# A convolution, attention and Mamba kernel: z projected in slots 25 and 27 of a Mamba step, and the convolutions' raw weights fetched two pieces ahead into two buffers

## The chip, the cores and the metric

The program runs on one core of one Trainium2 chip. A core has five engines that run side by side, each in the order of its own instruction stream: PE (TensorE, matrix products), DVE (VectorE), ACT (ScalarE), POOL (GpSimd) and SP (SyncE, which here only issues DMAs). The engines wait for each other by semaphores, and the DMA engines move data between the device's memory and the on-chip memory. The metric is the time in microseconds (us) on the device for one execution; less is better.

## The reference

The reference computes two layers on an image of 64 x 64 positions with 256 channels, all in float32.

- Layer 0 normalises the image in groups, makes q by a 1x1, k by a 3x3 and v by a 5x5 convolution, applies a depthwise 3x3 convolution to all three, and does attention over the 4096 positions in 8 heads of 32 channels.
- Layer 1 is a Mamba block that runs forward and backward over the 4096 positions, a small two-layer network, and then a mixture of 8 experts with one routing for the whole image.

Two places of it matter here. In layer 0, the k and v convolutions:

```
qkv = concat([conv(x, W1, 0), conv(x, W3, 1), conv(x, W5, 2)])
```

In layer 1, each direction of Mamba:

```
xz = einsum('bld,ed->ble', x, in_proj_w);  xc, z = split(xz, 2)
xc = silu(conv1d(xc) + conv_b);  dt, B, C = split(xc @ x_proj_w)
dt = softplus(dt @ dt_proj_w + dt_proj_b)
h_t = exp(dt * A) * h_{t-1} + dt * B * xc;   y_t = h_t . C_t
out = (y + xc * Dp) * silu(z) @ out_proj_w
```

The half of the input projection called z is used only at the end, as a gate on y.

## The kernel before, in words

The program goes through four phases: the convolutions (`conv_phase`), attention, Mamba (`mamba_phase`) and the experts. Inside each phase every engine runs its instructions in exactly the order in which the Python code issues them (`tc.manual_schedule`), so an instruction that has to wait holds back all that stands behind it on its engine. A DMA is issued by an engine too: those of SP and those of POOL form two queues, and a DMA that has to wait for a buffer or for data holds its queue.

**The convolutions.** k and v are computed by a transform method along the rows (Winograd's): the image, the weights and the result are each transformed by sums and differences on DVE, and PE forms the products. PE takes the work in units: (k, half of the image, half of the output channels), later v and q in turn. A unit of k has 6 products of 12 matmul instructions, one of v 8 products of 20 (`feed`, lines 421 to 464). `transform_out` (line 473) takes the products from PSUM: for a pair, ACT copies the second one into a scratch tile `c` (line 481), and DVE forms sum and difference in `out_t`. PE may run at most three products ahead of DVE.

The weights come in pieces, one for each kind, half of the output channels and row dy of the filter. There are 3 pieces of 384 KB for each half of k and 5 pieces of 640 KB for each half of v. `load_raw` (line 279) fetches a raw piece through POOL's DMA queue, `weights` (line 285) transforms it on DVE in two (k) or three (v) groups of instructions, and after each group POOL's queue stores two results of 128 KB to the device's memory (line 293). SP fetches them from there when PE needs them (line 430). When all pieces of a half are through, `ready` lets PE's feeding function use them.

The first three pieces, the first half of k, are fetched at the very start, two into other buffers and one into the buffer that all later pieces use. The pool `rp` has one buffer for each tag (line 195), so there is one buffer for a raw piece. The later 13 pieces are walked through by the generator `all_weights` (line 658): it fetches the first piece when it is first entered, and each further one after the last group of the piece before. `step_fill` (line 675) takes groups of weights and of input transforms in turn, a fixed number after each group of products, so that they fill DVE's time between the products. The order of all instructions is thus fixed in Python; only the waits between engines depend on the chip.

**Mamba.** The 4096 positions are cut into 8 chunks of 512, and each is done in both directions, which gives 16 steps i. A step has 32 slots, one for each tile of 128 x 1024 values of the state: 4 groups e of channels, 4 groups k of the state's index, and j = 0 or 2. In slot n (line 1753 on) POOL makes dbx two slots ahead (`inflow`), ACT makes exp(dt * A) one slot ahead (`decay`) and copies the last state of the slot before (`keep`), a one-element addition on ACT brings in the carried state (`bring`, line 1702), DVE runs the scan and multiplies by C (`recur`, lines 1682 and 1687), and PE sums the state's indices for a finished pair of slots (`sum_states`, line 1719).

Between these, each slot advances a generator `prepare(q)` (line 1267) by one part; it makes what the next step needs. But for the first step, its first three parts stand in slots 29, 30 and 31 of the step two before q, its fourth in slot 0, and its last in slot 29 of step q - 1. So the parts of a loop near its end, with `at` = 0 to 5 (line 1344), stand in slots 24 to 29. In this loop, `dt_piece` finishes a part of dt on POOL and sends it through SP to the device's memory, from where it is read back in a broadcast form for the next step. In the parts at = 0 and 2, `in_pair` projects two blocks of 128 channels of z on PE (8 matmul instructions at line 1249) into both of the two PSUM buffers with the tag mm. In the parts at = 1 and 3, ACT copies them to a tile z (line 1354). At the end of part 3, `load_u` puts the fetch of the input of the step after into SP's queue (line 1258). The tile u has a single buffer, so that this fetch has to wait until PE is through with the projection of z. Part 1 of the next `prepare`, in slot 29, projects from the new u.

A generator `tail(c)` does the small network for a finished chunk beside all this. It says at every stop which engine it needs next, and it goes on in a slot only if that engine isn't marked as full there. The table `FULL` holds these marks, written by hand (line 1739); among PE's marks are the two slots in which z is projected. A tail starts in every second step and stretches over about two, so that it begins its last layer norm in slots 24 to 28 of an odd step i.

Of the kernel before, what the change touches and what calls it, by code (L numbers as in the profile page):

```python
# [14 lines left out]
FP = mybir.dt.float32  # L15
# [9 lines left out]
P = 128  # L25
H = W = 64
NT = H * W
C = 256
CT = C // P
# [8 lines left out]
ET = DI // P  # L38
# [31 lines left out]
def drain(gen):  # L70
    while step(gen):
        pass
# [101 lines left out]
def conv_phase(cx, xT, w1, w3, w5, temp, qd, kd, vd, uk, uv):  # L174
# [17 lines left out]
    with ExitStack() as ctx:  # L192
        one = ctx.enter_context(tc.tile_pool(name="a_one", bufs=1))
        up = ctx.enter_context(tc.tile_pool(name="a_u", bufs=3))
        rp = ctx.enter_context(tc.tile_pool(name="a_r", bufs=1))
# [70 lines left out]
        KS = {"k": 3, "v": 5}  # L266
# [11 lines left out]

        def load_raw(kind, co, dy, pool=rp, tag="wr"):
            n = KS[kind]  # L280
            r = pool.tile([P, 5, C], FP, name="wr", tag=tag)
            nc.gpsimd.dma_start(out=r[:, 0:n, :], in_=RAW[kind][co, :, :, dy, :].rearrange("x p c -> p x c"))
            return r

        def weights(kind, co, dy, r):
            s = tp.tile([P, 2, C], FP, name="wx", tag="t")
            x, y = s[:, 0, :], s[:, 1, :]
            w = [r[:, i, :] for i in range(KS[kind])]

            def pair(i):  # L290
                o = tp.tile([P, 2, C], FP, name="wo", tag="t")
                return o, lambda: [
                    nc.gpsimd.dma_start(out=UD[kind][co][i + v - 1][:, dy, :], in_=o[:, v, :]) for v in range(2)
                ]

            o, store = pair(1)
            plus(x, w[0], w[2])
            if kind == "v":
                plus(y, w[1], w[3])
                plus(x, x, w[4])  # L300
            plus(o[:, 0, :], x, y if kind == "v" else w[1])
            plus(o[:, 1, :], x, y if kind == "v" else w[1], ALU.subtract)
            store()
            yield
            for i in (3, 5) if kind == "v" else (3,):
                o, store = pair(i)
                w_ = w if i == 3 else w[::-1]
                if kind == "k":
                    madd(x, w_[2], 4.0, w_[0])
                    odd = w_[1]  # L310
                else:
                    madd(x, w_[4], 4.0, w_[2])
                    madd(y, w_[3], 4.0, w_[1])
                    madd(x, x, 4.0, w_[0])
                    odd = y
                madd(o[:, 0, :], odd, 2.0, x)
                madd(o[:, 1, :], odd, -2.0, x)
                store()
                yield
# [98 lines left out]
        ready, us, ms, where = set(), {}, {}, {}  # L418
# [185 lines left out]

        with tc.manual_schedule(engines=ORDERED):
            raw = [load_raw("k", 0, dy, accp, "acc") for dy in range(2)] + [load_raw("k", 0, 2)]
            mv = one.tile([P, CT, 2], FP, name="mv")
            stats = one.tile([P, CT, NCH, 6], FP, name="stats")
            for t in range(CT):
# [39 lines left out]
            for b in range(3):  # L649
                normalise(b)  # L650
            drain(weights("k", 0, 2, raw[2]))
            ready.add(("k", 0))
            first = inputs("k", 0)
            for _ in range(2):
                step(first)
            normalise(3)

            def all_weights(pieces):
                r = load_raw(*pieces[0])
                for n, p in enumerate(pieces):  # L660
                    yield from (True for _ in weights(*p, r))
                    if n + 1 < len(pieces):
                        r = load_raw(*pieces[n + 1])
                    if p[2] == KS[p[0]] - 1:
                        ready.add(p[0:2])

            fills = [
                first, all_weights([("k", 1, dy) for dy in range(3)]), inputs("k", 1),
                all_weights([("v", 0, dy) for dy in range(5)]), inputs("v", 0),
                all_weights([("v", 1, dy) for dy in range(5)]), inputs("v", 1),  # L670
            ]

            pure = fills[1::2]
# [492 lines left out]
def mamba_phase(cx, early, w_in, w_x, w_out, w1, w2, x1d, ud, bcd, dtd, x2d, u2d, usum):  # L1166
# [12 lines left out]
    with ExitStack() as ctx:  # L1179
# [81 lines left out]
        def in_pair(q, e):  # L1261
            return [in_proj(q % 2, gots[q]["u"], e), in_proj(q % 2, gots[q]["u"], e + 1)]
# [4 lines left out]
        def prepare(q):  # L1267

            d, got = q % 2, gots[q]

            ps = in_pair(q, 0)
            yield
            xp = early.wide("xp")
            nc.scalar.copy(xp[:, :, 0:3], halo[d])
            for v in range(2):
                nc.scalar.copy(xp[:, v, 3:], ps[v])
            ps = in_pair(q, 2)
            yield
            for v in range(2):
                nc.scalar.copy(xp[:, 2 + v, 3:], ps[v])  # L1280
            nc.scalar.copy(halo[d], xp[:, :, N : N + 3])
            for _ in range(4):
                yield

            xc = None
            for e in range(ET + 1):
                if e > 0:
                    xc = got["xc"] = xc or pr.tile([P, ET, N], FP, name="xc", tag="xc")
                    nc.scalar.activation(xc[:, e - 1, :], ps, AF.Identity, bias=cx.col(f"convb{d}", e - 1))
                if e < ET:  # L1290
                    ps = mm_psum()
                    for k in range(4):
                        nc.tensor.matmul(  # L1293
                            ps, taps[d][:, 4 * e + k, :], xp[:, e, k : k + N], start=k == 0, stop=k == 3
                        )
                yield
            nc.scalar.activation(xc, xc, AF.Silu)
            yield
            ps = mm_psum()
            nx = DR + 2 * DS  # L1300
            for e in range(ET):
                nc.tensor.matmul(ps[0:nx, :], wx[d][:, e, :], xc[:, e, :], start=e == 0, stop=e == ET - 1)
            yield
            xd = few()[0:nx, :]
            nc.scalar.copy(xd, ps[0:nx, :])

            at = 0 if d else DR
            nc.sync.dma_start(out=bcd[q], in_=xd[at : at + 2 * DS, :])
            yield


            r = slice(32 * d, 32 * d + DR)
            ex = dt = None
            for e in range(ET + 1):
                if e > 0:
                    ex = early.wide("ex")[:, :, 0:N] if e == 1 else ex
                    dt = dt or sp.tile([P, ET, N], FP, name="dt", tag="dt")
                    nc.scalar.activation(ex[:, e - 1, :], ps, AF.Abs, bias=cx.col(f"dtb{d}", e - 1))
                    nc.scalar.activation(dt[:, e - 1, :], ps, AF.Relu, bias=cx.col(f"dtb{d}", e - 1))
                if e < ET:  # L1320
                    ps = mm_psum()
                    nc.tensor.matmul(ps, wdt[r, P * e : P * e + P], xd[r, :], start=True, stop=True)
                yield

            nc.scalar.activation(ex, ex, AF.Exp, scale=-1.0)
            yield
            rds, sums = {}, {}
            for e in range(ET + 2):
                if e < ET:
                    rd = rds[e] = few()  # L1330
                    nc.scalar.activation(rd, ex[:, e, :], AF.Identity, scale=-1.0, bias=-1.0)
                    nc.scalar.add(rd, rd, 1.0)
                if e > 1:
                    nc.scalar.copy(dt[:, e - 2, :], sums.pop(e - 2))
                if 0 < e <= ET:
                    ps = sums[e - 1] = mm_psum()
                    for v, x in enumerate((rds.pop(e - 1), ex[:, e - 1, :], dt[:, e - 1, :])):
                        nc.tensor.matmul(ps, cx.ident, x, start=v == 0, stop=v == 2)
                yield

            nc.scalar.activation(ex, ex, AF.Ln, bias=1.0)
            yield
            got["dt"] = dt
            for at, (v, e) in enumerate(((0, 0), (1, 0), (0, 1), (1, 1), (0, 2), (0, 3))):
                dt_piece(q, v, e, ex)
                if at == 4 and q > 1:
                    load_first(q, 0)
                if at in (0, 2):
                    zs = in_pair(q, ET + at)
                if at in (1, 3):  # L1350
                    z = sp.tile([P, 2, N], FP, name="z", tag="z", bufs=3)
                    got.setdefault("z", []).append(z)
                    for f in range(2):
                        nc.scalar.copy(z[:, f, :], zs[f])
                if at == 3 and q + 1 < 2 * NCH:
                    load_u(q + 1)
                yield
# [367 lines left out]
        def close(i, e):  # L1725
# [11 lines left out]
        LATE = {0: 0, 1: 0, 2: 0, 3: 0, 4: 0, 7: 5, 13: 2, 14: 2, 15: 2, 16: 2}  # L1737

        FULL = {
            "PE": {0, 1, 2, 3, 4, 5, 6, 7, 9, 18, 19, 20, 21, 24, 26, 29, 30},  # L1740
            "ACT": {0, 6, 7, 8, 16, 17, 18, 19, 20, 21, 22, 23, 30, 31},
            "POOL": {0, 1, 2, 4, 24, 25, 26, 27, 28, 29, 30, 31},
            "DVE": {8, 16},
# [3 lines left out]
        with tc.manual_schedule(engines=ORDERED):  # L1747
# [5 lines left out]
            for n, (i, e, k, j) in enumerate(slots):  # L1753
                at = n % SPS
# [391 lines left out]
```

## Time and profile before

| What | Value |
| --- | --- |
| Median of 3 runs | 4312.76 us (4305.44 to 4313.22) |
| Profiled execution, its own time | 4316.87 us |
| Its span, first to last instruction | 4315.0 us |
| PE busy | 3617.0 us (84%) |
| DVE busy | 3482.8 us (81%) |
| ACT busy | 2675.4 us (62%) |
| POOL busy | 1775.7 us (41%) |
| Granted TensorE clock, mean | 0.913 |
| Convolutions | 0 to about 725 us |
| Attention | about 725 to 2040 us |
| Mamba | about 2040 to 4000 us |
| Experts | about 4000 to 4315 us |

The profile is of one execution, so durations and waits are of that one, and sums are made against its own time. A line of a group says: source line, engine, operation, tile written and tiles read, shapes and count, then busy us and mean ns of one, then the idle time of the engine just before these instructions, with what ended it. A line of a time line says: start in us, length in us, engine, source line, operation, tiles, count, and in brackets the idle time before it with what ended it. SPq and POOL lines with a DMA operation are issues: the transfer itself goes on after them. Of several things that an instruction waits for, the profile names the one that came last by its own account, which can be the wrong one.

### The profile page before, as it was taken

The numbers are of one execution on the slowest core, as the hardware profiler recorded it, in microseconds if no ns is written. First come the engines' busy times: TensorE is split into PE (matmuls) and PEld (weight loads), VectorE is DVE, ScalarE is ACT, GpSimd is POOL, SyncE is SP. The second block draws the span as 40 slices with busy tenths as digits, with TensorE's granted clock in tenths as the row PEclk, the third lists the DMA queues.
The fourth block names the chain that finished last, engine by engine and source line by source line (L and its number), as shares of the span: only waits on it lengthen the run. The fifth ranks groups of instructions, "written<-read, shape, count | busy, mean of one in ns | idle before, by whom it ended". The sixth has DMA issues, their size and how long they took to land. (4 is left out here: it accounts for less than half of the span.)

```text
span 4315.0 us, 43522 instructions
## 1 busy us (share of the span) xinstructions
PE 3617.0 (84%) x15080; PEld 1184.1 (27%) x15080; DVE 3482.8 (81%) x2882; ACT 2675.4 (62%) x4176; POOL 1775.7 (41%) x1148
## 2 busy tenths in 40 slices
PE   4659895999999999998778787878888787876798
PEld 2214341222222222222222222222222222221343
DVE  6887876888888879778899998999999989999211
ACT  1012123888788788776777777777877777774122
POOL 2210000000000000000888888888888889897000
PEclk9879996999999999999888898989899898987799
DMA  4322124000000000002333433433334434432121
GB/s 148 126 81 90 68 91 130 4 20 22 21 26 11 25 22 21 11 18 84 106 114 114 125 121 114 128 114 117 110 106 122 128 114 121 121 110 85 64 64 38
DMA packets 150532, 351.18 MB, mean 81 GB/s; under 512 B 35493, under 2 KB 44453, under 8 KB 150046
## 3 DMA queue, kind: packets, MB, share of 16 engines
q1 hardware_dynamic: 139214, 313.17, 23.6%
q0 software_dynamic: 11088, 35.14, 2.4%
q8 instruction: 120, 1.97, 0.2%
q14 instruction: 110, 0.90, 0.1%
HBM read 268.69 MB, written 79.56 MB: 81 GB/s over the span
## 5 line engine op out<-in xcount | busy, mean ns | idle before, releaser
L1671 POOL TENSOR_TENSOR dbx<-dtxr,b 128x1024 f32<-128x1024 f32 x512 | 1202.1, 2359 | 202.6 <-DVE da L1682 125.4
L959 ACT ACTIVATE e<-sc 128x1024 f32<-128x1024 f32 x1024 | 992.8, 1023 | 205.6 <-PE sc L952 161.4
L1682 DVE TENSOR_TENSOR_SCAN da<-da,state,dbx 128x1024 f32<-128x1024 f32 x416 | 976.7, 2348 | 113.5 <-ACT dbx L1702 66.4
L880 DVE TENSOR_TENSOR s<-s,e 128x1024 f32<-128x1024 f32 x768 | 880.4, 1214 | 43.9 <-ACT e L959 43.3
L1661 ACT ACTIVATE da<-dtr,aneg 128x512 f32<-128x512 f32 x1024 | 708.1, 692 | 59.9 <-DVE h L1682 27.7
L952 PE MATMUL sc<-q,kS 32*128 32x512 f32 x4096 | 653.9, 644 | 21.3 <-DMA kS<-kd 11.5
L132 POOL TENSOR_TENSOR ln_few<-ln_few,minus_half 128x4 f32<-128x4 f32 x29 | 29.4, 1013 | 1415.7 <-DMA ln_few<-ln_row 1415.7
L887 PE MATMUL av<-e,vT 128*32 128x512 f32 x4096 | 549.6, 608 | 3.7 <-ACT o L893 3.7
L1687 DVE TENSOR_TENSOR h<-da,c 128x1024 f32<-128x1024 f32 x416 | 509.4, 1225 | 34.5 <-PE y L1719 4.0
L452 PE MATMUL cv<-v,u 128*128 128x512 f32 x928 | 420.8, 614 | 63.7 <-DVE pad L272 27.2
L1719 PE MATMUL y<-h,sel 128*32 128x512 f32 x2048 | 374.0, 653 | 100.9 <-DVE h L1687 73.5
L1249 PE MATMUL mm<-u,win 128*128 128x512 f32 x496 | 271.8, 704 | 96.3 <-DMA u<-ud 83.9
L952 PEld LDWEIGHTS sc<-q,kS 32*128 32x128 f32 x4096 | 211.3, 184 | 467.7 <-issue 243.4
L452 PEld LDWEIGHTS cv<-v,u 128*128 128x128 f32 x928 | 181.5, 198 | 301.5 <-issue 229.8
L528 DVE SCALAR_TENSOR_TENSOR acc<-pad,wdw_s,acc 128x768 f32<-128x768 f32 (+1 forms) x192 | 244.5, 1279 | 19.4 <-ACT acc L524 13.3
L1682 DVE TENSOR_TENSOR_SCAN h<-da,state,dbx 128x1024 f32<-128x1024 f32 x96 | 224.9, 2343 | 15.5 <-ACT da L1661 6.3
L1692 POOL TENSOR_TENSOR h<-h,c 128x1024 f32<-128x1024 f32 x96 | 226.1, 2355 | 2.1 <-ACT state L1710 2.1
L1293 PE MATMUL mm<-xp,taps 128*128 128x512 f32 x480 | 213.7, 597 | 11.2 <-DVE m L1440 11.2
L1710 ACT COPY state<-da 128x2 f32<-128x2 f32 x415 | 65.3, 157 | 241.4 <-DVE h L1687 240.6
L880 DVE TENSOR_TENSOR s<-e 128x1024 f32<-128x1024 f32 x128 | 150.7, 1217 | 72.1 <-ACT e L959 71.9
L887 PEld LDWEIGHTS av<-e,vT 128*32 128x32 f32 x4096 | 81.3, 108 | 396.8 <-issue 379.2
L1249 PEld LDWEIGHTS mm<-u,win 128*128 128x128 f32 x496 | 108.4, 227 | 267.2 <-issue 147.8
(347 smaller groups left out, 3822.8 us busy)
## 6 DMA issues: line engine op xcount, KB each, us to landing
dtr<-dtd SPq DMA_DIRECT2D x128, 512.0 KB
dtxr<-dtd SPq DMA_DIRECT2D x128, 512.0 KB
b<-bcd SPq DMA_DIRECT2D x64, 256.0 KB
c<-bcd SPq DMA_DIRECT2D x64, 256.0 KB
dtd<-dt SPq DMA_DIRECT2D x64, 256.0 KB
dtd<-few SPq DMA_DIRECT2D x64, 256.0 KB
u<-uv SPq DMA_DIRECT2D x24, 640.0 KB
u<-ud SPq DMA_DIRECT2D x16, 512.0 KB
```

The lines of the kernel that those rows point to most:

```text
L452: nc.tensor.matmul(rows4(ps), u[:, dy, P * ci : P * ci + P], v[:, dy : dy + HR, ci, :], start=dy + ci == 0, stop=dy == k - 1 and ci == CT - 1,
L528: nc.vector.scalar_tensor_tensor(o, src, w_ap, o, ALU.mult, ALU.add)
L880: nc.vector.tensor_tensor(z, x, y, ALU.add)
L887: nc.tensor.matmul(g.av[32 * h : 32 * h + 32, :], vT[:, kb, P * t + 32 * h : P * t + 32 * h + 32], es[h // 2][:, h % 2, :], start=kb == 0, ...
L952: nc.tensor.matmul(ps[h // 2][:, h % 2, :], kS[r, t, P * kb : P * kb + P], q_t[r, t, :], start=True, stop=True,)
L959: nc.scalar.activation(e, ps[i], AF.Exp)
L1249: nc.tensor.matmul(ps, win[d][:, t, P * e : P * e + P], u[:, t, ::-1] if d else u[:, t, :], start=t == 0, stop=t == CT - 1,)
L1661: nc.scalar.activation(da[:, v, :], dts[i, e, j][0][:, v, :], AF.Exp, scale=aneg[i % 2][:, a : a + 1])
L1671: nc.gpsimd.tensor_tensor(u, dts[i, e, j][1], bcs[i, k][0][:, None, :].to_broadcast([P, 2, N]), ALU.mult)
L1682: nc.vector.tensor_tensor_scan(das[n].rearrange("p v n -> p (v n)"), da.rearrange("p v n -> p (v n)"), u.rearrange("p v n -> p (v n)"), st ...
L1687: nc.vector.tensor_tensor(h, da, bcs[i, k][1][:, None, :].to_broadcast([P, 2, N]), ALU.mult)
L1719: nc.tensor.matmul(ys[i, e][32 * j : 32 * j + 32, :], cx.sel, hs[n + j // 2][:, j % 2, :], start=False, stop=k == SQ - 1,)
```

## The change

In the convolutions, the tag of the raw pieces gets two buffers in the pool `rp`. A list `ahead` holds the pieces that are fetched and not yet used. One of the 13 later pieces is fetched at the very start, behind the first three; a second one after the third piece has been transformed. From then on each piece that has been transformed is followed by the fetch of the piece two after it, over the borders between the halves and kinds as well. The order of all DVE instructions stays.

In Mamba, the parts that project z move from at = 0 and 2 to 1 and 3 (slots 25 and 27), and the parts that copy it from 1 and 3 to 2 and 4 (slots 26 and 28). The fetch of the next u stays at the end of part 3, which now also holds the second projection of z, ahead of it. In `FULL`, PE's marks move from slots 24 and 26 to 25 and 27.

```diff
-            r = pool.tile([P, 5, C], FP, name="wr", tag=tag)
+            r = pool.tile([P, 5, C], FP, name="wr", tag=tag, bufs=2 if pool is rp else None)
...
             raw = [load_raw("k", 0, dy, accp, "acc") for dy in range(2)] + [load_raw("k", 0, 2)]
+            pieces = [("k", 1, dy) for dy in range(3)] + [("v", co, dy) for co in range(CT) for dy in range(5)]
+            ahead = [load_raw(*pieces.pop(0))]
...
             drain(weights("k", 0, 2, raw[2]))
+            ahead.append(load_raw(*pieces.pop(0)))
...
-            def all_weights(pieces):
-                r = load_raw(*pieces[0])
-                for n, p in enumerate(pieces):
-                    yield from (True for _ in weights(*p, r))
-                    if n + 1 < len(pieces):
-                        r = load_raw(*pieces[n + 1])
-                    if p[2] == KS[p[0]] - 1:
-                        ready.add(p[0:2])
+            def all_weights(kind, co):
+
+                for dy in range(KS[kind]):
+                    yield from (True for _ in weights(kind, co, dy, ahead.pop(0)))
+                    if pieces:
+                        ahead.append(load_raw(*pieces.pop(0)))
+                ready.add((kind, co))
...
-                if at in (0, 2):
-                    zs = in_pair(q, ET + at)
                 if at in (1, 3):
+                    zs = in_pair(q, ET + at - 1)
+                if at in (2, 4):
                     z = sp.tile([P, 2, N], FP, name="z", tag="z", bufs=3)
...
-            "PE": {0, 1, 2, 3, 4, 5, 6, 7, 9, 18, 19, 20, 21, 24, 26, 29, 30},
+            "PE": {0, 1, 2, 3, 4, 5, 6, 7, 9, 18, 19, 20, 21, 25, 27, 29, 30},
```

More of the change, by code (lines that the diff above doesn't have):

```diff
@@ L656, in conv_phase @@
             normalise(3)
-            def all_weights(pieces):
-                r = load_raw(*pieces[0])
-                for n, p in enumerate(pieces):
-                    yield from (True for _ in weights(*p, r))
-                    if n + 1 < len(pieces):
-                        r = load_raw(*pieces[n + 1])
-                    if p[2] == KS[p[0]] - 1:
-                        ready.add(p[0:2])
+            def all_weights(kind, co):
[4 more added lines that the diff above has]
+                ready.add((kind, co))
             fills = [
-                first, all_weights([("k", 1, dy) for dy in range(3)]), inputs("k", 1),
-                all_weights([("v", 0, dy) for dy in range(5)]), inputs("v", 0),
-                all_weights([("v", 1, dy) for dy in range(5)]), inputs("v", 1),
+                first, all_weights("k", 1), inputs("k", 1),
+                all_weights("v", 0), inputs("v", 0),
+                all_weights("v", 1), inputs("v", 1),
             ]
```

## The prediction

> **What bounds the kernel now.** I read the page first (span 4315.0 us), then the busy time by stage, because no engine is full all the way. Columns: us, then busy us and count of PE, PEld, DVE, ACT, POOL, then granted TensorE clock, DMA share, GB/s.
>
> ```profile
> 0.00:310.00 310.00, 164.29 (x340) 67.34 (x341) 238.72 (x395) 36.93 (x50) 65.09 (x125) 0.82 0.37 122
> 310.00:725.00 415.00, 344.30 (x851) 144.68 (x849) 319.28 (x299) 91.47 (x136) 26.16 (x53) 0.90 0.22 76
> ...
> 2040.00:4000.00 1960.00, 1547.65 (x4342) 504.41 (x4341) 1779.27 (x1077) 1440.47 (x2799) 1662.59 (x947) 0.88 0.38 115
> ```
>
> The convolution's first 310 us and the Mamba phase belong to DVE; the convolution from 310 us leans on PE. The two halves of the change fall into the two DVE stages. For the first I asked for the groups up to 450 us; the line below is the first instruction of a weight piece:
>
> ```profile
> L275 DVE TENSOR_TENSOR wx<-wr 128x256 f32<-128x256 f32 x26 | 10.1, 419 | 39.5 <-DMA wr<-in_w 33.6 <-issue 5.9
> ```
>
> DVE stands still 39.5 us because a raw piece has not landed. The time line of DVE has the nine places (start, length, idle before):
>
> ```profile
> 77.98 0.42 DVE L275 TENSOR_TENSOR wx<-wr 128x256 f32<-128x256 f32 x1 [4.76 <-DMA wr<-in_w]
> ...
> 96.95 0.76 DVE L275 TENSOR_TENSOR wx<-wr 128x256 f32<-128x256 f32 x2 [3.09 <-DMA wr<-in_w]
> ...
> 105.17 1.29 DVE L275 TENSOR_TENSOR out_t<-cv,c 128x512 f32<-128x512 f32 x2 [2.48 <-ACT c L481]
> ...
> 161.29 0.76 DVE L275 TENSOR_TENSOR wx<-wr 128x256 f32<-128x256 f32 x2 [5.99 <-DMA wr<-in_w]
> ...
> 209.79 0.76 DVE L275 TENSOR_TENSOR wx<-wr 128x256 f32<-128x256 f32 x2 [5.90 <-issue]
> ```
>
> The others are 85.14 (4.69), 149.50 (0.52), 222.31 (1.49), 235.20 (7.08) and 269.83 (5.96). The "issue" one is the same line and has the same size. The time line of POOL, then of PE, shows why a fetch is late and where PE is the judge:
>
> ```profile
> 73.18 1.07 POOL L293 DMA_DIRECT2D uk<-wo  x2 [9.39 <-DVE wo L272]
> 74.24 0.75 POOL L282 DMA_DIRECT2D wr<-in_w  x1
> ```
> ```profile
> 91.80 43.61 PE L452 MATMUL cv<-v,u 128*128 128x512 f32 x96 [13.89 <-DMA u<-uk]
> ```
>
> The fetch follows the last store of the piece before, so DVE sees its whole flight (3.6 to 8.3 us to landing, median 4.8).
>
> For Mamba I took the time lines around the end of a step (slot = one scan). Step 5, SP queue, ACT and DVE; step 4, PE:
>
> ```profile
> 2761.11 0.63 SPq L1379 DMA_DIRECT2D dtd<-few  x1
> 2763.02 0.32 SPq L1258 DMA_DIRECT2D u<-ud  x1
> ```
> ```profile
> 2761.31 0.58 ACT L1354 COPY z<-mm 128x512 f32<-128x512 f32 x1 [2.10 <-PE mm L1249]
> 2763.02 0.58 ACT L1354 COPY z<-mm 128x512 f32<-128x512 f32 x1 [1.13 <-PE mm L1249]
> ```
> ```profile
> 2766.18 2.36 DVE L1682 TENSOR_TENSOR_SCAN da<-da,state,dbx 128x1024 f32<-128x1024 f32 x1 [1.92 <-ACT dbx L1702]
> ...
> 2778.77 2.36 DVE L1682 TENSOR_TENSOR_SCAN da<-da,state,dbx 128x1024 f32<-128x1024 f32 x1 [1.72 <-ACT dbx L1702]
> ```
> ```profile
> 2633.11 3.70 PE L1249 MATMUL mm<-u,win 128*128 128x512 f32 x8
> ...
> 2647.32 2.90 PE L1249 MATMUL mm<-u,win 128*128 128x512 f32 x3 [7.10 <-DMA u<-ud]
> ```
>
> Two waits per step: scan 29 waits because ACT stands in the second pair of z copies, and the next step's first scan waits for a chain: u fetched, next step's in-projection on PE, its xp copies on ACT, decay and dbx behind them.
>
> **What the Trainium skill says.** "DMA: Bandwidth & Descriptors", Rules for kernel authors: issue a DMA early and wait on it late, and its fixed cost overlaps; that is the first half of the change. The same page, Anatomy of one DMA, puts a GpSimd-issued DMA at about 2.0 us plus bytes / 436 GB/s: an estimate of 3.5 us for 640 KB. The trace's 4.8 median is used. The section adds that a semaphore wait is held by the issuing sequencer, not by the DMA engines: so a u fetch that waits on PE holds SP's later fetches, as the trace shows at 2763.02. "TensorE: Matmul & The Clock Gate", Part 1: an idle window of about 3.4 us halves the clock. The trace agrees: after the 13.89 us wait the granted clock is 0.50 from 91.8 to 96 us and 1.00 from 98.
>
> **The raw weights, step by step.** Pieces p0 to p2 are ("k",1), p3 to p7 ("v",0), p8 to p12 ("v",1). Removed: no DVE work, only waits. Added: one fetch in flight and 5 KB a partition.
> - Start: one more 384 KB fetch among the input loads, with the queues at 370 to 406 GB/s up to 18 us: at most 1.0 us later; bn_stats already waits for the last loads. I take +0.7 (0 to 1.0).
> - p1 (61.5 to 77.98): fetched at 33, no wait, -4.76. p2's fetch leaves where p1's left (74.24) and lands near 78; p1 now ends at 73.2 + 2.4 = 75.6, so p2 still waits 2.3. Gain here 4.76 + 4.69 - 2.3 = 7.1.
> - p3: its wait of 3.09 goes, but the next instruction, out_t at 105.17, waits for PE's second product. ACT's wait before it is put down to a store, yet 24 matmuls of 0.45 us from 91.80, with some 2 us lost at half clock, end at 104.5: PE. PE starts when p2's transformed weights are back, 7.1 earlier. So the 3.09 turns into wait for PE: gain 0.
> - p6 0.5, p7 6.0, p9 5.9, p10 1.5, p11 7.1, p12 6.0. Each fetch now leaves a whole piece earlier; the tightest is p7's, out at about 137.6 on the new clock and needed at 147.7, against 8.3 us for the slowest flight. What follows each finds its product: PE is idle before these (18.31 us at 216.18, 17.45 at 272.98, both for DVE). Sum 27.0.
> - The POOL queue gets no new wait: a fetch needs the buffer of the piece just finished, whose last store stands just ahead of it. Six scratch buffers of tag t still suffice: a store lands 2.0 us after issue, its buffer returns at least 6 us later.
>
> Sum: -7.1 - 27.0 + 0.7 = -33.4. From 298 us PE works on what DVE delivers (22.00 us wait there for pad), so the shift passes through the PE-led part unshortened.
>
> **z one slot later.** Work is equal; 15 steps (0 to 14) prepare a successor. Even steps: no tail work for PE lies at slots 24 to 27, so PE's order is the same; z's first eight matmuls stay. Their two copies (1.1 us) go behind keep, decay and dbx of the next slot, so the second eight start near 2634.6 instead of 2633.11 and end near 2638.5. The u fetch (same slot 27, now behind z in the same call) leaves at 2640.91 anyway, since it is queued behind the dtd stores that POOL releases at 2640.06: about 2 us of cover. Gain 0. If the cover is gone, each us costs 14 us in all (14 fetches of u). SP's b, c, first_r and dtr/dtxr fetches are queued behind it; ACT and POOL need them in the next step.
>
> Odd steps with a tail (3, 5, 7, 9, 11, 13): FULL now lets the tail's PE work (L113, after DVE's m) go at slot 24, before z instead of between its pairs. I estimate PE at step 5: L113 from 2750.4, z1 from 2752.5, y sums, z2 about 2758 to 2762 (was 2759.3 to 2763.0); u leaves up to 1.2 earlier, at some steps 0.2. The z copies stand behind decay and dbx of slot 29, so the wait before scan 29 (1.70 to 1.95 in these six, 10.7 in all) goes. But the next step's first scan still waits for the u chain: DVE arrives 1.8 earlier and waits that much longer, less u's gain. I take 0.5 x 6 = -3, bounded by -11 (the whole wait stays away) and +6 (1 us late in six).
>
> Total -33.4 - 3 = -36.4. Against the profiled execution, 4316.87 (span 4315.0, 1.9 around it): 4280.5. The runs' median lies 4.1 lower at 4312.76: **4276**.
>
> **Rivals.**
> 1. Mamba keeps more: the u chain has slack and the 10.7 stays won, 4312.8 - 33.4 - 10.7 = 4269. For it: step 13 has no wait at the next first scan. Against: the other five wait 0.75 to 2.1 there.
> 2. PE becomes the bound in the convolution, as it does for p3: half of the later 27 turns into waits for products, 4312.8 - 7 - 13.5 + 0.7 - 3 = 4290. For it: 105.17 already waits. Against: PE's idle gaps of 8.4 to 22 us afterwards.
> 3. Slower: z's second pair falls in a cold clock. Matmuls then take twice the time (3.7 becomes 7), it starts 2 us later, and u leaves 3 or more after its old time; 14 x 3.2 = 45 eats the 36: 4321. It decides from 36.4 / 14 = 2.6 us of lateness a step to break even. Against: the idle gap before it is 1 to 2 us, under the window.
> 4. The fetches stay late (the second buffer is not free when wanted) and nothing is gained: about 4312. Against: its reader is the piece just done.
>
> **How the numbers follow.** Forecast 0.68, rival 1 0.12, rival 2 0.10, rival 3 0.06, rival 4 0.04. Two tenths of a per cent (8.6 us, about what runs of this kernel can tell) gives faster 0.90, same 0.04, slower 0.06. The range, 4265 to 4293, holds most of the forecast (4268 to 4286), rival 1's upper half and rival 2.
>
> **What would show it.** Idle before wx<-wr falls from 39.5 to 2 or 3 us; out_t near 98 us waits some 5.6 for ACT c; the 17.45 and 22 us waits of PE shrink by their share of 27; the convolution ends 33 earlier. In Mamba no wait before scan 29 in odd steps, a longer one before the next first scan, u leaving no later. Wrong if waits on wr remain beyond p2, if DVE's waits for c grow beyond p3's, or if u leaves later in even steps.

## The result, and the profile after

The changed kernel takes 4273.62 us (median of 4 runs, 4266.57 to 4276.95) against 4312.93 for the kernel before beside it (4 runs, 4305.44 to 4313.22). The ratio is 0.9914, with an interval of 0.9901 to 0.9928: 37 us (31 to 43) less by the ratio. On another chip the same two kernels gave 0.9917 (0.9900 to 0.9934). The forecast was 4276.

The profiled execution after took 4276.95 us, its span is 4275.1 us. The stages by busy time come first, cut where the same work begins and ends (columns as for before):

```profile
0.00:277.00 277.00, 157.06 (x334) 64.95 (x334) 232.56 (x391) 34.86 (x46) 65.11 (x125) 0.84 0.42 136
277.00:692.00 415.00, 346.47 (x858) 145.92 (x856) 322.48 (x290) 92.75 (x140) 25.07 (x51) 0.91 0.21 72
...
2007.00:3967.00 1960.00, 1556.01 (x4372) 507.36 (x4371) 1787.54 (x1089) 1446.58 (x2809) 1663.48 (x948) 0.88 0.38 116
```

The first stage is 33 us shorter with nearly the same work in it: DVE is busy 232.6 of 277 us where it was busy 238.7 of 310. The groups of instructions up to 450 us have the wait itself:

```profile
L275 DVE TENSOR_TENSOR wx<-wr 128x256 f32<-128x256 f32 x26 | 10.0, 417 | 2.7 <-DMA wr<-in_w 2.7
```

39.5 us of idle time before these instructions became 2.7. The time line of DVE shows the one wait for a raw piece that is left, p2's, and the place that stood at 105.17 before:

```profile
80.64 0.42 DVE L275 TENSOR_TENSOR wx<-wr 128x256 f32<-128x256 f32 x1 [2.68 <-DMA wr<-in_w]
...
105.31 1.29 DVE L275 TENSOR_TENSOR out_t<-cv,c 128x512 f32<-128x512 f32 x2 [10.30 <-ACT c L481]
```

p2 waits 2.68 (2.3 was forecast). But the transform at 105.31 starts no earlier than before, after a wait of 10.30 instead of 2.48: in this pair of profiles the first 7 us gained are lost again there. The time line of PE shows the same start as before (91.80), and where the gain appears later:

```profile
91.79 43.77 PE L452 MATMUL cv<-v,u 128*128 128x512 f32 x96 [11.53 <-DMA u<-uk]
...
245.66 3.78 PE L444 MATMUL cv<-xpad,wq 128*128 128x512 f32 x4 [13.67 <-DVE out_t L275]
271.44 3.78 PE L444 MATMUL cv<-xpad,wq 128*128 128x512 f32 x4 [22.01 <-DVE pad L272]
```

The third group of matmuls of the q convolution ("q's third group" from here on) stands at 271.44, where it stood at 298.76: 27.3 earlier, against 27.0 that the forecast had for the pieces from p6 on. Its wait is still put down to DVE, and the last product of the convolution ends 28.4 earlier (635.3, before 663.7).

POOL's queue tells why PE got nothing out of the first 7 us in this pair. The lines are issues, uk<-wo the stores of transformed weights, wr<-in_w the raw fetches:

```profile
79.48 0.88 POOL L282 DMA_DIRECT2D wr<-in_w  x1
81.82 0.56 POOL L293 DMA_DIRECT2D uk<-wo  x1 [1.46 <-DVE wo L275]
82.67 1.60 POOL L293 DMA_DIRECT2D uk<-wo  x3 [0.29 <-DVE wx L272]
84.26 0.87 POOL L282 DMA_DIRECT2D wr<-in_w  x1
```

p2's stores leave at 81.8, 4.5 earlier than before (86.33), but now behind p3's raw fetch of 640 KB, issued at 79.48, and with p4's right after them. The trace's answer for the tile uk from 81 to 98 us gives the time from a store's issue to its landing, for before and for after:

```profile
DMA to landing us min/median/max: 2.0/2.0/2.8
```
```profile
DMA to landing us min/median/max: 3.1/3.4/4.1
```

The first of p2's stores lands at 85.91, 4.1 after its issue (before: 88.34, 2.0 after). SP then fetches u at 86.03, and PE starts 5.76 later; before, it was 88.45 and 3.35. So 4.5 us of lead shrink to 2.4 at the landing and to nothing at PE. Two passages of the Trainium skill, "DMA: Bandwidth & Descriptors", fit: within one queue of a DMA engine descriptors start in order (section Two DMAs through the same engine are not ordered), so a small store has a large fetch ahead of it; and the DMA engines go round between queues packet by packet (section Queues, rings and completion order), so the fetch of u shares them with p4. No run here shows the order inside a queue or the turns of an engine. What the traces show is the load: between 82 and 92 us the queues moved 289 GB/s after, 167 before. In the 3 us from about the first fetch of u on, SP's queue, which carries u, moved 0.23 MB after (86 to 89 us) and POOL's 0.61; before it was 0.46 and 0.27 (88.4 to 91.4 us).

For Mamba, step 5 again, at its end: DVE, SP's queue, ACT and PE (PE: the tail's L113, the second z projection, the next step's in-projection).

```profile
2730.70 2.33 DVE L1685 TENSOR_TENSOR_SCAN da<-da,state,dbx 128x1024 f32<-128x1024 f32 x1
...
2745.10 2.36 DVE L1685 TENSOR_TENSOR_SCAN da<-da,state,dbx 128x1024 f32<-128x1024 f32 x1 [3.55 <-ACT dbx L1705]
```
```profile
2728.26 0.43 SPq L1382 DMA_DIRECT2D dtd<-few  x1
2729.51 0.32 SPq L1260 DMA_DIRECT2D u<-ud  x1
```
```profile
2730.29 1.05 ACT L1357 COPY z<-mm 128x512 f32<-128x512 f32 x2
```
```profile
2716.87 2.79 PE L113 MATMUL tl<-m,mean_mat 128*128 128x512 f32 x4 [2.89 <-DVE m L1483]
...
2725.77 3.70 PE L1251 MATMUL mm<-u,win 128*128 128x512 f32 x8
...
2736.11 9.94 PE L1251 MATMUL mm<-u,win 128*128 128x512 f32 x16 [3.72 <-ACT da L1664]
```

Scan 29 (2730.70) has lost its wait of 1.92, since ACT's z copies at 2730.29 now stand behind decay and dbx. But u leaves only when z's second projection is through (2729.47), so it leaves 1.1 after the start of scan 28, as before, and the next first scan waits 3.55 instead of 1.72. In this step the wait has moved and little is won, as forecast. In the even step 4 the second projection of z ends at 2604.5 and u leaves at 2607.16, right behind the dtd stores, with 2.6 us of cover (forecast: about 2).

From profile to profile the 39.9 us build up so: -28.4 at the end of the convolution, -24.4 at Mamba's first scan, -43.3 at Mamba's last scan, -39.9 at the end. The 4 us lost in and around attention are within the scatter of that stretch: the changed kernel's own two profiles (e10 has the second) have 1384.8 and 1375.9 us for it. The -18.9 in Mamba can't be believed as it stands either: see the experiments.

### The profile page after: what moved, and what is told of

Read it like the earlier page. It is cut to its first block, busy times and chain, and to the rows that moved or that the text cites. A ratio compares the mean times of both kernels' runs of the same rounds, so it can differ in the third digit from the quotient of the medians.

```text
span 4275.1 us, 43538 instructions
## 1 busy us (share of the span) xinstructions
PE 3614.0 (85%) x15080; PEld 1184.8 (28%) x15080; DVE 3484.1 (81%) x2882; ACT 2674.4 (63%) x4176; POOL 1775.6 (42%) x1148
## 5 line engine op out<-in xcount | busy, mean ns | idle before, releaser
L1251 PE MATMUL mm<-u,win 128*128 128x512 f32 x496 | 262.1, 683 | 94.8 <-DMA u<-ud 59.1
```

Of the source, the lines that this page charges most:

```text
L1251: nc.tensor.matmul(ps, win[d][:, t, P * e : P * e + P], u[:, t, ::-1] if d else u[:, t, :], start=t == 0, stop=t == CT - 1,)
```

## The experiments

Three sets, each on one chip with the kernel before beside it. "After" is the changed kernel.

### The two halves, and the halves of the second (e1 to e4)

e1 has the raw weights' half alone, e2 the whole Mamba half alone. e3 moves z but leaves FULL as it was; e4 moves only PE's marks in FULL:

e1, the core of its edit (the fetches as in the diff of the change; Mamba as before):

```diff
-            r = pool.tile([P, 5, C], FP, name="wr", tag=tag)
+            r = pool.tile([P, 5, C], FP, name="wr", tag=tag, bufs=2 if pool is rp else None)
...
+            ahead = [load_raw(*pieces.pop(0))]
```

e3, which is e2 without its line in FULL:

```diff
-                if at in (0, 2):
-                    zs = in_pair(q, ET + at)
                 if at in (1, 3):
+                    zs = in_pair(q, ET + at - 1)
+                if at in (2, 4):
```

e4, which is e2's line in FULL alone:

```diff
-            "PE": {0, 1, 2, 3, 4, 5, 6, 7, 9, 18, 19, 20, 21, 24, 26, 29, 30},
+            "PE": {0, 1, 2, 3, 4, 5, 6, 7, 9, 18, 19, 20, 21, 25, 27, 29, 30},
```

> The raw weights' half alone (two buffers, two pieces ahead), z and FULL as before. Theory A (the trace after: the convolution gives 27 to 28, Mamba the rest): q's third group of matmuls at 271 to 272 us, the convolution's end near 635, 27 to 28 us less than before in all, Mamba's 16 steps as long as before (1946 us from first to last scan, odd steps 736). Theory B (the prediction as written): 33 us less. Theory C (raw weights change Mamba too, by moving it in time): Mamba shorter than 1940.

> The Mamba half alone (z in slots 25 and 27, FULL's marks with it). Theory A: 10 to 13 us less than before, all in the six odd steps with a tail (736 to about 724), no wait before scan 29 there, u's flight 7.8 to about 5.8 us. Theory B: 3 us less; the u chain takes the gain back. Theory D (the two profiles differ by chance of 10 us in Mamba): between.

> z in slots 25 and 27, but FULL's marks stay at 24 and 26, so that the tail's work stays where it was and the x2d store still leaves some 9 to 10 us after scan 24 begins. Theory E (the earlier tail frees the DMA queues for u): scan 29's waits of 1.7 to 1.9 go, u's flight stays near 7.8, the wait before the next first scan grows, gain 0 to 4 us. Theory F (the z copies out of ACT's way are what counts): gain 9 to 12 us as with both.

> Only FULL's marks move, z stays in slots 24 and 26: the tail's products, its x2d store and its norm come a slot earlier. Theory E: u's flight in odd steps falls from 7.8 to about 6, gain 5 to 10 us, scan 29's waits mostly stay or shrink as z's second pair comes earlier on PE. Theory F: u's flight as before, gain under 3 us.

| Kernel | Median, us | Ratio to before (4306.22, 52 runs) | In us |
| --- | --- | --- | --- |
| e1, raw weights alone | 4274.22 | 0.9925 (0.9912 to 0.9939) | -32 (-38 to -26) |
| e2, z and FULL | 4301.26 | 0.9989 (0.9981 to 0.9997) | -5 (-8 to -1) |
| e3, z without FULL | 4311.77 | 1.0009 (1.0001 to 1.0017) | +4 (0 to +7) |
| e4, FULL alone | 4297.61 | 0.9983 (0.9975 to 0.9990) | -7 (-11 to -4) |

The halves add up: -32 and -5 make -37, the whole change's ratio gives -37. Nearly all of it is the raw weights. In the Mamba half the named act, moving z, doesn't pay by itself; what pays is the new marks, by which the tail may use PE in slots 24 and 26 and no longer in 25 and 27. The intervals of e2 and e4 overlap; by the means of their 21 and 16 runs e2 is 4.0 us slower (0.7 to 7.3), so moving z costs a little on top of the marks.

Of the expectations, e1's interval holds both the 27 to 28 of Theory A and the 33 of Theory B. e2 rules out Theory A's 10 to 13. e3 came out slower, where both of its theories had a gain or nothing. e4 gains what Theory E said, but the part of E that u's flight stays near 7.8 without the marks failed: e3 has 6.0.

In the trace, e1 has the convolution of after: q's third group at 270.55, idle time before wx<-wr 2.6. For Mamba the four profiles, those of before and after, and those of later runs give the following; the six steps are the odd ones from 3 to 13, all in us:

| Profile of | Waits before scan 29, six steps | Waits at the next first scan, six steps | Length of the six steps | First to last scan |
| --- | --- | --- | --- | --- |
| before | 10.7 | 6.7 | 736.1 | 1945.7 |
| before again (e9) | 10.2 | 0.3 | 732.0 | 1929.5 |
| e1 (Mamba as before) | 11.0 | 2.0 | 729.3 | 1933.8 |
| e3, z without FULL | 0 | 6.4 | 725.0 | 1929.6 |
| e2, z and FULL | 0 | 7.4 | 725.0 | 1931.7 |
| after | 0 | 4.8 | 724.1 | 1926.8 |
| after again (e10) | 0 | 2.8 | 719.6 | 1927.0 |
| e4, FULL alone | 0 | 2.9 | 718.5 | 1918.5 |
| e8, raw weights and FULL | 0 | 2.6 | 723.9 | 1930.3 |
| e11, the same | 0 | 8.1 | 728.3 | 1928.5 |

Three things follow. First, either edit takes the whole wait before scan 29 away. With FULL alone the tail's L113 no longer holds up z's second projection: that ends 3.3 before the start of scan 28 instead of about there. In e4's step 5, PE and then DVE (scan 28):

```profile
2739.82 1.88 PE L113 MATMUL tl<-m,mean_mat 128*128 128x512 f32 x4
...
2743.76 3.70 PE L1249 MATMUL mm<-u,win 128*128 128x512 f32 x8
```
```profile
2750.81 2.34 DVE L1682 TENSOR_TENSOR_SCAN h<-da,state,dbx 128x1024 f32<-128x1024 f32 x1
```

Before, L113 started at 2753.88, z's second projection ended at 2762.99, and scan 28 started at 2761.92. Second, little of the wait comes back at the next first scan: those waits average 3.0 in the first three rows and 5.0 in the others, and rows of one kernel differ by more than that (0.3 and 6.7 for the kernel before). Against my forecast, the six steps stay some 9 us shorter (732.5 on average in the first three rows, 723.5 in the rest). Third, by the medians not all of this reaches the end. One loss is plain: in step 14, every profile with z moved has a new wait before scan 30 (after, time line of DVE):

```profile
3823.22 2.35 DVE L1685 TENSOR_TENSOR_SCAN da<-da,state,dbx 128x1024 f32<-128x1024 f32 x1 [3.77 <-issue]
```

The kernels with z in its old slots have a shorter one behind that scan (2.74 in before); slots 29 and 30 together take 11.0 to 11.6 us against 9.0 to 10.2. What else makes e3 slower than e4 is not settled. By the medians it is 14 us. The 11 us from first to last scan rest on e4's one profile: e7, e8 and e11, with the same Mamba code as e4, took 1928.5 to 1930.3, as long as e3. And e3's profile is of an execution that took 4303.86, 8 us less than its median. The waits at the first scan after an even step alone add up to between 19 and 28 us a profile, over kernels of both kinds.

### Where the first 7 us went (e5, e6)

One pair of profiles is little to go by. Ten profiles have either the old fetches (before, e2, e3, e4, e9) or those of the change (after, e1, e8, e10, e11):

| Start of, us | Old fetches: range, mean | New fetches: range, mean | Means |
| --- | --- | --- | --- |
| DVE's first input transform | 33.08 to 34.27, 33.48 | 34.34 to 34.77, 34.50 | +1.0 |
| First of p2's stores, issue | 86.33 to 88.22, 87.27 | 81.25 to 81.86, 81.64 | -5.6 |
| First fetch of u after it, issue | 88.45 to 90.36, 89.40 | 84.74 to 86.03, 85.50 | -3.9 |
| PE, from that u | 91.80 to 93.77, 92.74 | 90.05 to 91.85, 90.92 | -1.8 |
| q's third group | 298.76 to 301.53, 299.97 | 270.23 to 271.44, 270.70 | -29.3 |
| End of the convolution | 663.7 to 666.9, 665.4 | 634.5 to 636.1, 635.5 | -29.9 |

So of the first 7 us some 2 reach PE on average, and 27.5 more are gained between PE's start and q's third group. The 29.9 at the end agrees with the 32 (26 to 38) by e1's times.

Two causes were in question for what PE doesn't get: the raw fetches beside p2's stores, and the input loads at the start, which have one more fetch beside them. e5 holds p3's fetch back until p2 has been transformed (p4 and p5 then follow p3). e6 takes the extra fetch out of the start: p0 is fetched where the kernel before first fetched a later piece, and p1 right behind it (33.07 and 33.94 in the trace, not near 61 as expected). Both are edits of after, run once each.

e5:

```diff
-                    if pieces:
+                    if pieces and (kind, co, dy) != ("k", 1, 1):
+                        ahead.append(load_raw(*pieces.pop(0)))
+                    if (kind, co, dy) == ("v", 0, 0):
                         ahead.append(load_raw(*pieces.pop(0)))
```

e6:

```diff
-            ahead = [load_raw(*pieces.pop(0))]
+            ahead = []
...
             def all_weights(kind, co):
-
+                if kind == "k":
+                    ahead.append(load_raw(*pieces.pop(0)))
```

> The changed kernel, but the fetch of p3 is held back until p2 is transformed, and p4's and p5's until p3 is: POOL's queue then has no 640 KB fetch ahead of p2's stores. Theory G (the raw fetch ahead in POOL's own queue makes p2's stores land 4.1 us after issue instead of 2.0, and slows the u fetch behind them): the store issued near 82 lands 2.0 to 2.3 us later, PE starts its seventh product near 87.5 instead of 91.8, the third out_t comes at 101 instead of 105.3, and q's third group 4 us before 271.4. Theory H (PE or ACT sets that start anyway): both stay where they are.

> The changed kernel without the fetch at the very start: p0 is fetched after the third piece (at 33 us), p1 when p0's turn comes (near 61 us). If the extra fetch at the start costs what the sum put at 0.7 (0 to 1.0) us, the first v<-xpad on DVE goes from 34.8 back to 33.1 to 34.1 us, and the later dates with it; p1 has landed long before it is needed, so no new wait for wr. If the delay at the start is chance, 34 to 35 stays.

e5 took 4269.19, e6 4272.98 (before: 4303.8, 11 runs); the time lines say more than single times. In e5 a store of uk takes 2.0 to 2.7 us to land again. Its answer for the tile uk from 81 to 98 us, its time line of DVE, then of PE:

```profile
DMA to landing us min/median/max: 2.0/2.2/2.7
```
```profile
92.31 0.76 DVE L275 TENSOR_TENSOR wx<-wr 128x256 f32<-128x256 f32 x2 [3.51 <-DMA wr<-in_w]
100.72 1.29 DVE L275 TENSOR_TENSOR out_t<-cv,c 128x512 f32<-128x512 f32 x2 [2.68 <-ACT c L481]
```
```profile
86.69 44.27 PE L452 MATMUL cv<-v,u 128*128 128x512 f32 x96 [7.08 <-DMA u<-uk]
...
266.87 3.48 PE L444 MATMUL cv<-xpad,wq 128*128 128x512 f32 x4 [22.01 <-DVE pad L272]
```

p3 now waits 3.51 for its raw piece, as it must, and that costs nothing: PE starts at 86.69 instead of 91.79, the transform stands at 100.72 instead of 105.31, and q's third group is 4.6 earlier. Against all five profiles with the new fetches, PE starts 3.4 to 5.2 earlier and q's third group stands 3.4 to 4.6 earlier; e7, which has the same edit, has PE at 85.16. So the traffic of the raw fetches was the cause of most of what was lost between DVE and PE. e5 takes away both at once, the fetch ahead of the stores and the one ahead of u, and doesn't tell how they share the loss.

For the start, first the time line of DVE in after, then in e6:

```profile
15.26 1.29 DVE L613 BATCH_NORM_STATS2 stats<-v 128x6 f32<-128x512 f32 x2 [0.72 <-DMA v<-in_xT]
17.47 3.91 DVE L613 BATCH_NORM_STATS2 stats<-v 128x6 f32<-128x512 f32 x6 [0.93 <-DMA v<-in_xT]
...
34.77 2.49 DVE L272 SCALAR_TENSOR_TENSOR v<-xpad 128x1088 f32<-128x1088 f32 x2 [1.05 <-ACT xpad L647]
```
```profile
14.41 5.30 DVE L613 BATCH_NORM_STATS2 stats<-v 128x6 f32<-128x512 f32 x8 [0.16 <-DMA v<-in_xT]
...
33.09 2.49 DVE L272 SCALAR_TENSOR_TENSOR v<-xpad 128x1088 f32<-128x1088 f32 x2 [1.04 <-ACT xpad L647]
```

In after, the statistics wait 0.72 and 0.93 for the last inputs and the first transform starts at 34.77; without the extra fetch it is 33.09, as in before (33.08). These single profiles make it 1.7 us. The table's means make it 1.0, where I had taken 0.7 and at most 1.0; and the start varies without the extra fetch too (34.27 in e3). q's third group is 2.7 earlier in e6 than in after, 1.5 to 2.7 against the five profiles with the new fetches.

### All gains together (e7), and z put back (e8)

e7 has the edits of e5 and e6 and that of e8. e8 is after with z back in slots 24 and 26, and keeps FULL's new marks:

```diff
+                if at in (0, 2):
+                    zs = in_pair(q, ET + at)
                 if at in (1, 3):
-                    zs = in_pair(q, ET + at - 1)
-                if at in (2, 4):
```

> A candidate: the raw weights' half with both of these (p3 to p5 held back, nothing extra at the start), FULL's marks moved, z left in slots 24 and 26. Sum of the parts, if they add: 32 us for the raw weights, 7 for FULL alone, 4 for the held fetches, 1.5 for the start: 44 us less than before, 7 less than the changed kernel. If the held fetches only move the wait, 39.

> The changed kernel with z put back into slots 24 and 26, FULL's marks left in their new place. If moving z costs time once the tail is out of its way (the u fetch leaves later), 2 to 4 us less than the changed kernel, 39 less than before; if z's place doesn't matter, as the changed kernel, 36 to 37 less than before.

e7: 4271.13 (6 runs), ratio 0.9918 (0.9902 to 0.9934). e8: 4269.04 (5 runs), ratio 0.9916 (0.9901 to 0.9930), both to the same runs of before. For e7, 44 us or 39 less were expected, and 35 less (28 to 42) were measured, so 44 is out. In e7's trace q's third group is at 264.58, 5.7 to 6.9 earlier than in the five profiles with the new fetches, but the last product of the convolution ends at 631.6, only 2.9 to 4.5 earlier: in the stage that leans on PE a third to a half of this further gain is given back. The time shows nothing of the rest. A well understood 4 us in the convolution did not make a kernel that is measurably faster.

### Before and after once more (e9 to e11)

e9 is the kernel before, e10 the changed kernel, e11 is e8 again, on one chip: for a second profile of both kernels, and to decide between z in its old and new slots.

> The kernel before once more, for a second profile of the very same program. If the 18.9 us by which Mamba was shorter in the profile after is the change's, Mamba takes 1946 us here again (odd steps 736). If some 12 of it was the one execution's, as the profile of the raw weights alone says (1933.8, odd steps 729), it takes 1930 to 1940.

> The changed kernel again, on the same chip as the next one: 36 to 38 us less than before.

> The raw weights and FULL's marks, z in slots 24 and 26, on the same chip. If z's later slots cost 3 to 5 us by themselves, as they did against the kernel before, this is 3 to 5 us under the changed kernel; if not, the two are within 2 us.

e9 took 4305.82 (one run); e10 4268.93 (5 runs), ratio 0.9917 (0.9900 to 0.9934); e11 4266.37 (4 runs), ratio 0.9906 (0.9887 to 0.9925). e11 and e10 differ by 2.6 us and their intervals overlap, so no version was found that surely beats the changed kernel, and on top of the raw weights the cost of moving z is not shown. The group of the Mamba scans, in the first profile of the kernel before and in e9's, shows what one profile is worth:

```profile
L1682 DVE TENSOR_TENSOR_SCAN da<-da,state,dbx 128x1024 f32<-128x1024 f32 x416 | 976.7, 2348 | 113.5 <-ACT dbx L1702 66.4 <-ACT state L1710 30.2 <-ACT da L1661 15.8
```
```profile
L1682 DVE TENSOR_TENSOR_SCAN da<-da,state,dbx 128x1024 f32<-128x1024 f32 x416 | 976.7, 2348 | 97.9 <-ACT dbx L1702 58.4 <-ACT state L1710 28.0 <-ACT da L1661 11.6
```

The same code, the same busy time, and 15.6 us less idle. The profile that the forecast was read from was long by itself in Mamba: 1945.7 us from first to last scan, against 1929.5 in e9 and 1933.8 in e1, which has the same Mamba code. Of the 18.9 us between the two first profiles, 12 to 16 are this.

## Why the prediction was right, and where it was not

The total was right (4276 forecast, 4273.62 measured, range 4265 to 4293), and the main term held: the waits of the later pieces, 27.0 by the sum, are 27.3 in the first pair of traces and 27.5 by the means of five and five, and the shift passed through the PE-led part, as said (29.3 at q's third group, 29.9 at the convolution's end). Point by point:

- **Start, +0.7.** Right as far as the profiles tell: 1.0 by the means, at my upper bound, though the first pair has 1.7.
- **p1 and p2, -7.1.** This step failed. DVE's waits did go (4.76 and 4.69 became nothing and 2.68), but I let PE's start move with DVE's work. Between them stand p2's stores and the fetch of u, which have 640 KB fetches ahead of them and beside them once fetches run early: landing 3.4 to 4.1 instead of 2.0, the fetch of u 5.0 to 5.9 instead of 3.3 to 3.4. With the later start, nothing was left of 7.1 in the first pair and 1.8 by the means; e5 brings 3.4 to 5.2 of it back. I had it that "The POOL queue gets no new wait" and that "a store lands 2.0 us after issue": the first is true of the issues, but the landing is not a constant. The trace before already has 2.0 to 3.9 for v's stores.
- **p3, gain 0.** Right: its 3.09 became wait for PE, 10.30 in all, since in this pair PE itself came no earlier.
- **p6 to p12.** Right, with no wait on wr left. The stores land later there too (v's stores up to 5.1 us after issue, before up to 3.9), but PE was waiting on DVE's inputs.
- **z, even steps, 0.** Right on the queue: z's second projection begins where I put it (10.7 after scan 24, I had 10.8) and u stays gated by the dtd stores. Step 14, which prepares no further u, has a new wait that I did not see, about 1.7 us net.
- **z, odd steps, -3.** The size is within the measured half (-5, -8 to -1), the working behind it only in part. The wait before scan 29 did go. I said that it comes back at the next first scan; step 5 shows it, but over the six steps only about 2 of 10.6 return on average, which is within the scatter. u leaving "up to 1.2 earlier" failed: on average over the six steps it leaves 0.55 and 0.63 us after the start of scan 28 in the two profiles of after, in three with the old Mamba code 0.24 and 0.75 after it and 0.54 ahead of it. What is shorter is the way from u's issue to the in-projection: 5.3 to 5.8 instead of 6.2 to 7.8. The tail's own store leaves SP's queue some 4 us earlier with the new marks, which could be why, but e3 has the old marks and 6.0, so this is only argued.
- **Which edit gains.** I put the gain on moving z with FULL as a help; the runs show FULL's marks as the gain, and the move of z as a small cost: 4 us by e3 alone and by e2 against e4, nothing certain on top of the raw weights (e10, e11).

Rival 1 (Mamba keeps 10.7) is out for the timed half: its interval ends at -8. Rival 2 (PE bound in the convolution) took hold only where the forecast had it anyway, at p3, and for gains beyond the 27 (e7). Rival 3 did not occur: z's second projection takes 3.70 us in every step, as before, after at most 1.3 us of idle time. Rival 4 is excluded by the 2.7 us left on wr. That the total fits by 2 us is partly luck: the sum had 5.0 us too much gain in the convolution by the first pair (-33.4 against -28.4), 3.5 by the means, and some 2 too little in Mamba, and runs of one kernel lie some 10 us apart.

## What to carry to other kernels

Fetching early removes the reader's wait, but the early fetches run at another time: look at which small, urgent transfers now stand behind or beside them, above all stores and reloads on the way to another engine, and put those first. When an edit has a schedule move and a change of marks or priorities in it, run them apart; in the Mamba half the part that was named last was the one that gained. And before reading a difference of some 10 us from two profiles, take a second profile of both kernels: here the first pair said that nothing of 7 us was left and that Mamba had won 19 us, and neither held.

## What was not expected of the hardware

- A 128 KB store issued 2.2 to 2.6 us behind a 640 KB fetch in the same queue took 3.4 to 4.1 us to land in five profiles, instead of 2.0.
- The order of issue of two fetches in different queues shows in the times of both. With a 640 KB fetch issued 1.1 to 1.8 us ahead of it, the first fetch of u took 5.0 to 5.9 us until PE started. With the 640 KB fetch issued 0.2 to 0.3 us behind it (the old fetches, e5 and e7) it took 3.3 to 3.5, and the 640 KB fetch landed only after 8.3 to 9.4 us, instead of 5.2 to 6.4.
- The same program scatters from 4296.6 to 4319.6 us over 52 runs on one chip, and its Mamba part by 16 us between two profiles, with the same busy time on DVE.
